# Depthwise stage with partitions ordered (q/k/v, chunk, channel), stores cut to the parts that are read, and constants loaded on GpSimd's queue

## The chip, the cores and the metric

One core of one Trainium2 chip. The metric is the device time of the whole kernel in microseconds, given as the median of several runs. A profiled execution, taken by the hardware profiler, stands beside the runs.

Engines in the text: PE (TensorE), DVE (VectorE), ACT (ScalarE), POOL (GpSimd) and SP (SyncE), which here only issues DMAs. ACT and POOL issue DMAs too.

## The reference

Input x is one image of 48 channels, 256 by 256, in float32. Two layers, each with a residual:

```python
x = x + attention(group_norm(x))
x = x + mix(group_norm(x))

def attention(x):
    qkv = einsum('bchw,oc->bohw', x, w_qkv)        # 48 -> 144 channels
    qkv = depthwise_3x3(qkv, w_dw)
    q, k, v = split(qkv, 3)                        # 48 channels each
    # unfold in 4x4 patches: 64*64 inner patches (and a border of zeros)
    q, k, v = (heads(unfold(t)) for t in (q, k, v))  # 8 heads x 96 x n
    q, k = l2norm(q, over the 96), l2norm(k, over the 96)
    attn = softmax(einsum('bhcn,bhcm->bhnm', q, k) * temperature)
    out = einsum('bhcn,bhnm->bhcm', v, attn)
    return einsum('bchw,oc->bohw', fold(out), w_proj)
```

`mix` multiplies 64 by 64 windows from three sides with three sets of matrices (Ws, Hs, Cs) and adds the three results. A head has 6 channels of q, 6 of k and 6 of v; with the 16 pixels of a patch these are its 96 rows. There are 4096 inner patches, so each head has a 4096 by 4096 attention matrix.

## The kernel before

The kernel runs in stages.

**Head of the kernel.** Constants are loaded (lines 81 to 111): `gm`, `wq`, `wr`, `wp` and `tb` on ACT's queue (14 loads), `dwt`, the depthwise weights, in 21 loads on SP's queue, one for each of 3 parts and 7 chunks. Then x is loaded into SBUF in ten pieces for each half of the image (L424), the upper half on SP and the lower on ACT. DVE takes the statistics of each piece as it arrives (`bn_stats`, L428), then the group norm is folded into `wq` and `wr` and a bias. The pointwise convolution of heads 0 and 1 follows (`pointwise`, L158), and its result is written to a DRAM tensor `t1[0]` (L475). The other six heads' pointwise convolution is done later, in 64 strips of two rows per half (class `Strip`), in the course of head 0's attention; it writes `t1[1]`.

**Depthwise convolution** (class `Depthwise`). For one head h and one step r of ten, 126 partitions hold 7 chunks of the image (index j) times 18 channels of the head: 6 of q, 6 of k, 6 of v. A chunk is 36 image rows; a step takes four of them, with a row above and one below. `load` brings that to the tile `pad`, `first` and `tap` (or `taps_on_tensor`) form the nine taps, `square`, `reduce` and `norm` give the squared norms, summed over the 6 channels of a part by a matmul with the mask `same`; `root` and `scale` divide by them. `nmul` and `nadd` are per-partition constants that give q the temperature and leave v alone. `high` and `low` split the result o in two float32r parts, oh and ol, so that the logits can be computed from three float32r products. `store` writes three tensors to DRAM, `qkv[h][0]` from oh, `qkv[h][1]` from ol and `qkv[h][2]` from o. Each is written with all 126 partitions. Later only q and k are read from the first two (`load_queries`, `load_keys`) and only v from the third (`load_value`). Each partition writes 16 runs of 64 floats.

**Head 0's depthwise stage** (`depthwise_first`) runs alone, before the attention. The pads of steps 0 and 1 are loaded chunk by chunk, alternating between SP and ACT; the other steps with one DMA each on SP. Six of the ten steps have their taps on PE, the other four on DVE. Of their stores oh goes to SP, ol to POOL and o to SP, and for the last two steps oh and ol to SP and o to POOL. The loads of keys and queries for the attention come after these stores, as they read the same DRAM tensor.

**Attention.** A head has 16 groups of two blocks of 128 queries. A block has 48 matmuls for its logits (L344), four exponentials on ACT (L563), and its weighting of the values (`weigh`, L592). The order within a group is written out by hand (`tc.manual_schedule()`). Into it are laid the depthwise steps of the next head, one step in flight in each of the stages `load`/`first`, taps, and `store`; in head 0 also the strips. Pads are loaded on SP, and the three stores are issued on POOL.

**Rest.** After head 7 the projection with the first residual (L739), and then the second layer.

Outside the hand-ordered parts the framework orders each engine's instructions. A DMA has one of eight completion semaphores of the hardware queues (SP and ACT together) or one of eight of POOL's; the next DMA on a semaphore is issued when the one before it has landed.

Of the kernel before, what the change touches and what calls it, by code (L numbers as in the profile page):

```python
# [8 lines left out]
F32 = mybir.dt.float32  # L9
# [11 lines left out]
KS = 4  # L21
KK = KS * KS
NH = 8
HD = C * KK // NH
# [4 lines left out]
CH = 7  # L29
CR = 9  # L30
HC = 3 * C // NH
NP1 = CH * HC
PX = W // KS
H0 = 2
M0 = H0 * HC
# [9 lines left out]
def conv_preact_kernel(  # L45
# [15 lines left out]
    nc = tc.nc  # L61
# [4 lines left out]
    dram = ctx.enter_context(tc.tile_pool(name="dram", bufs=1, space=DRAM))  # L66
# [5 lines left out]
    TR = 2 * CR * KS + (CH - 1) * CR * KS  # L72
    CN = CR * PX
    t1 = [dram.tile([(h1 - h0) * HC, TR, W + 2], F32, name=f"t1_{h0}") for h0, h1 in GROUPS]
    qkv = [dram.tile([3, CH, HC * KK, CN + PX], F32, name=f"qkv{h}") for h in range(NH)]

    os_ = dram.tile([NT // TP, C * KK, TP], F32, name="os_")
    x1s = dram.tile([C, H, W], F32, name="x1s")
# [4 lines left out]
    ones = const.tile([C, 128], F32, name="ones")  # L83
    nc.vector.memset(ones, 1.0)
    gm = const.tile([P2, P2], F32, name="gm")
    nc.scalar.dma_start(out=gm, in_=gmat)

# [3 lines left out]
    wp = const.tile([P2, P2], F32, name="wp")  # L93
    nc.vector.memset(wp, 0.0)
    for s in range(2):
        r = slice(s * C, (s + 1) * C)
        for h in range(NH if s == 0 else H0):
            o = s * M0 + h * HC if h < H0 else (h - H0) * HC
            nc.scalar.dma_start(
                out=(wq[r] if h < H0 else wr[0:C])[:, o : o + HC].rearrange("c (z e) -> c z e", z=3),  # L100
                in_=w_qkvT.rearrange("c (z h e) -> h c z e", z=3, h=NH)[h],
            )
        nc.scalar.dma_start(out=wp[r, r], in_=w_projT)
    dwt = const.tile([NP1, NH, 9], F32, name="dwt")
    dws = w_dw.rearrange("(z h e) i a b -> z e h (i a b)", z=3, h=NH)
    for z in range(3):
        for j in range(CH):
            p = j * HC + z * 6
            nc.sync.dma_start(out=dwt[p : p + 6], in_=dws[z])
    tb = const.tile([1, NH], F32, name="tb")  # L110
    nc.scalar.dma_start(out=tb, in_=temp.rearrange("h a b -> (a b) h"))


    tabs = const.tile([1, 2], F32, name="tabs")
# [55 lines left out]
    class Strip:  # L170
# [5 lines left out]
        def load(self):  # L176
            self.xs = cv.tile([64 + C, 2, W], F32, name="xs", bufs=3)
            for s, rows in enumerate(both_halves(xc, 2 * self.j, 2)):
                nc.sync.dma_start(out=self.xs[s * 64 : s * 64 + C], in_=rows)
# [19 lines left out]
    class Depthwise:  # L199
# [6 lines left out]
        def load(self, engs=None):  # L206
            g = [i for i, (h0, h1) in enumerate(GROUPS) if h0 <= self.h < h1][0]
            c0 = (self.h - GROUPS[g][0]) * HC
            self.pad = self.pool.tile([NP1, KS + 2, W + 2], F32, name="pad", bufs=2 * self.bufs)
            rows = t1[g][c0 : c0 + HC, self.r * KS : self.r * KS + CH * CR * KS, :]  # L210
            rows = rows.rearrange("c (j y) x -> j c y x", j=CH)[:, :, : KS + 2, :]
            if engs:
                for j in range(CH):
                    engs[j % len(engs)].dma_start(out=self.pad[j * HC : (j + 1) * HC], in_=rows[j])
            else:
                nc.sync.dma_start(out=self.pad, in_=rows)

        def first(self):
            self.acc = self.pool.tile([NP1, KS, W], F32, name="acc", bufs=2)
# [79 lines left out]
        def store(self, parts=(0, 1, 2), eng=nc.gpsimd):  # L299
            px = slice(self.r * PX, (self.r + 1) * PX)  # L300
            for i in parts:
                eng.dma_start(  # L302
                    out=qkv[self.h][i].rearrange("j (c k) n -> (j c) k n", k=KK)[:, :, px],
                    in_=self.o if i == 2 else (self.ol if i else self.oh).bitcast(F32),
                )


# [13 lines left out]

    def load_keys(kt, h, m, eng=nc.sync):
        col = m * 512, (m + 1) * 512
        k0, k1 = (qkv[h][i, :, HD : 2 * HD] for i in range(2))
        to = kt.bitcast(F32)
        load(to[0:HD, 0, :], k0, *col, eng)
        load(to[HD:128, 0, :], k1[:, 0:32], *col, eng)
        load(to[0:64, 1, :], k1[:, 32:], *col, eng)
        load(to[64:128, 1, :], k1[:, 32:], *col, eng)

    def load_queries(qt, h, g):
        col = g * 256, (g + 1) * 256
        to = qt.bitcast(F32)
        for i in range(2):
            qi = qkv[h][i, :, 0:HD]
            load(to[0:HD, i, :], qi, *col)
            load(to[HD:128, i, :], qi[:, 0:32], *col)
            load(to[i * 64 : (i + 1) * 64, 2, :], qi[:, 32:], *col)
# [70 lines left out]
    with tc.tile_pool(name="xn", bufs=1) as xnp, tc.tile_pool(name="cst", bufs=1) as cst, tc.tile_pool(  # L409
        name="nps", bufs=2, space=PSUM  # L410
    ) as nps, tc.tile_pool(name="pw", bufs=4, space=PSUM) as pw:
        zr = cst.tile([128, W + 2], F32, name="zr")
        nc.gpsimd.memset(zr, 0.0)
        for (h0, h1), t in zip(GROUPS, t1):
            for y in (0, H + 1):
                nc.gpsimd.dma_start(out=t[:, y, :], in_=zr[: (h1 - h0) * HC])
        xr = xnp.tile([P2, HALF, W], F32, name="xr")
        parts = [16] * 7 + [8, 4, 4]
        st0 = cst.tile([P2, HALF * W // 512, 6], F32, name="st0")
        for i, LR in enumerate(parts):  # L420
            j = sum(parts[:i])
            for s in range(2):
                eng = nc.sync if s == 0 else nc.scalar
                eng.dma_start(  # L424
                    out=xr[s * C : (s + 1) * C, j : j + LR, :], in_=xc[:, s * HALF + j : s * HALF + j + LR, :]
                )
            for i in range(0, LR, 2):
                nc.vector.bn_stats(st0[:, (j + i) // 2, :], xr[:, j + i : j + i + 2, :].rearrange("p a b -> p (a b)"))  # L428
        group_stats(st0, mean0, rstd0, cst, nps)

        nc.vector.tensor_scalar_mul(wq, wq, rstd0)
        nc.vector.tensor_scalar_mul(wr[0:C], wr[0:C], rstd0[0:C])
        nc.gpsimd.dma_start(out=wr[64 : 64 + C], in_=wr[0:C])
        for g, (w, k) in enumerate(((wq, P2), (wr, C))):
            m = w.shape[1]
            pb = nps.tile([128, 1], F32, name="pb0", tag="pstat")
            nc.tensor.matmul(pb[:m], lhsT=w[:k], rhs=mean0[:k], start=True, stop=True)
            nc.vector.tensor_scalar_mul(bias[:m, g : g + 1], pb[:m], -1.0)

        pick = cst.tile([2 * CH, NP1], F32, name="pick")  # L440
        nc.vector.memset(pick, 0.0)
        nc.vector.tensor_copy(
            pick.rearrange("k (j z c) -> k j z c", j=CH, z=3)[:, :, 0:2],
            ident[: 2 * CH, : 2 * CH]
            .rearrange("k (j z u) -> k j z u", j=CH, u=1)
            .to_broadcast([2 * CH, CH, 2, 6]),
        )
        pk = nps.tile([NP1, NP1], F32, name="pk", bufs=1)
        nc.tensor.matmul(pk, lhsT=pick, rhs=pick, start=True, stop=True)
        nc.vector.tensor_copy(same, pk)  # L450
        row = cst.tile([1, NH + 1, NP1], F32, name="row")
        rv = row.rearrange("u i (j z c) -> u i j z c", j=CH, z=3)
        nc.vector.memset(row, 0.0)
        for i in range(NH):
            nc.vector.tensor_copy(
                rv[:, i, :, 0, :], tb[:, i : i + 1].rearrange("u (j c) -> u j c", j=1).to_broadcast([1, CH, 6])
            )
        nc.vector.memset(rv[:, :NH, :, 1, :], 1.0)
        nc.vector.memset(rv[:, NH, :, 2, :], 1.0)
        pr = nps.tile([NP1, NH + 1], F32, name="pr", bufs=1)  # L460
        for i in range(NH + 1):
            nc.tensor.matmul(pr[:, i : i + 1], lhsT=row[:, i, :], rhs=ones[0:1, 0:1], start=True, stop=True)
        nc.vector.tensor_copy(nmul, pr[:, :NH])
        nc.vector.tensor_copy(nadd, pr[:, NH : NH + 1])

        OR = 8
        for y in range(0, HALF, OR):
            ot = xnp.tile([2 * M0, OR, W + 2], F32, name="ot0", bufs=4)
            nc.gpsimd.memset(ot[:, :, 0:1], 0.0)
            nc.gpsimd.memset(ot[:, :, W + 1 : W + 2], 0.0)  # L470
            for i in range(0, OR, 2):
                ps = pw.tile([128, 512], F32, name="pw")
                pointwise(ps, ot[:, i : i + 2, :], xr[:, y + i : y + i + 2, :], on_vector=(i // 2 % 2 == 1))
            for s, rows in enumerate(both_halves(t1[0], y, OR, base=1)):
                nc.sync.dma_start(out=rows, in_=ot[s * M0 : (s + 1) * M0])  # L475
# [11 lines left out]
    with tc.If(nc.values_load(large) > 0):  # L487
# [8 lines left out]
        with tc.tile_pool(name="mk", bufs=NM) as mk, tc.tile_pool(name="mq", bufs=2) as mq, tc.tile_pool(  # L496
            name="mps", bufs=2, space=PSUM
# [23 lines left out]
    with tc.tile_pool(name="ahead", bufs=2) as ah, tc.tile_pool(name="ae", bufs=3) as ae, tc.tile_pool(  # L521
# [15 lines left out]
        def load_value(h, m):  # L537

            vt = ah.tile([HD, 4 * 128], F32, name="vt")
            load(vt, qkv[h][2, :, 2 * HD :], m * 512, (m + 1) * 512)  # L540
            values[h, m] = vt

        def turn(h, m):
# [414 lines left out]
```

## Time and profile before

| | us |
|---|---|
| median of 3 runs | 3771.0 |
| lowest and highest | 3754.03 and 3777.11 |
| the profiled execution's own time | 3774.41 |
| its span, first to last instruction | 3772.6 |
| PE busy | 3521.1 (93%) |
| DVE busy | 2185.9 (58%) |
| ACT busy | 1715.5 (45%) |
| POOL busy | 597.5 (16%) |

A line of the profile's groups or of its timeline names an engine, a line of the kernel and the operation with its output and inputs. Entries with a q after the engine (SPq, ACTq) are DMA issues on that engine's queue. In brackets stands the idle time ahead of an instruction and what ended it. In the table by stage, the last three columns are the granted clock of PE, the mean busy share of the core's 16 DMA engines, and the GB/s that they moved.

### The profile page before, as it was taken

Reading aid. Unit: us, or ns where it says so; the run is one execution under the profiler, and the core shown is the slowest. Engines: PE = TensorE matmul, PEld = TensorE weight load, DVE = VectorE, ACT = ScalarE, POOL = GpSimd, SP = SyncE. Lnnn points to the kernel's source line nnn. Section 1 sums busy time; section 2 is a strip of 40 time slices with the busy share of each in tenths; the row PEclk is TensorE's granted clock in tenths of the full one; section 3 lists DMA queues with packets and bytes.
Section 4 is the critical chain, followed back from the end, with each engine's and each line's share of the span. In section 5 each row is a group of like instructions: output and inputs, shape, how many; then the busy total and the mean of one; then the engine's idle time right before and its main releaser. Section 6 shows DMA issues by size and latency. Waiting matters only on the chain.

```text
span 3772.6 us, 100069 instructions
## 1 busy us (share of the span) xinstructions
PE 3521.1 (93%) x44252; PEld 2916.8 (77%) x44252; DVE 2185.9 (58%) x3514; ACT 1715.5 (45%) x2667; POOL 597.5 (16%) x593
## 2 busy tenths in 40 slices
PE   1877999999999999999999999999999999955998
PEld 0335777788888888888888888888888888812776
DVE  5463675169727962896299439934992222256664
ACT  0224565555545554555455445545554444300222
POOL 0031121012301220122122112211221100010011
PEclk9988999999999999999999999999999999966999
DMA  6575666534433542354245424542543100199784
GB/s 144 170 172 159 178 192 177 166 111 118 114 83 99 126 113 73 104 125 107 84 106 122 101 77 113 119 104 75 125 114 93 46 19 23 31 242 199 128 145 91
DMA packets 307826, 441.64 MB, mean 117 GB/s; under 512 B 98474, under 2 KB 232954, under 8 KB 303160
## 3 DMA queue, kind: packets, MB, share of 16 engines
q1 hardware_dynamic: 253668, 269.65, 27.7%
q0 software_dynamic: 48320, 156.61, 18.5%
q10 hardware_dynamic: 5396, 8.88, 1.1%
q8 instruction: 351, 5.75, 0.7%
q14 instruction: 91, 0.75, 0.1%
HBM read 234.76 MB, written 199.95 MB: 115 GB/s over the span
## 4 chain that ended last, share of the span: by engine, by line
PE 84%; DMA 5%; issue 2%; ACT 0%; SPq 0%; DVE 0%; POOL 0%; ACTq 0%; POOLq 0%
PE big L344 37%; PE big L592 36%; PE pb L856 4%; PE pa L834 2%; PE pc L873 2%; PE big L185 2%; DMA x1s<-pxt 1%; DMA pxt<-in_x_dram 1%; DMA t<-ot 1%; PE pt L609 1%; PE pst L546 1%; PE pn L258 1%; DMA kt<-qkv 0%; DMA os__70<-oo 0%; DMA lxq<-x1s 0%
## 5 line engine op out<-in xcount | busy, mean ns | idle before, releaser
L563 ACT ACTIVATE e<-big,nmx 128x1024 f32<-128x1024 f32 x1024 | 1143.9, 1118 | 833.8 <-PE big L344 622.4
L344 PE MATMUL big<-kt,qt 128*128 128x512 f32 x6144 | 1438.9, 393 | 44.4 <-DMA qt<-qkv 31.6
L592 PEld LDWEIGHTS big<-vn,e 128*64 128x64 f32 x32768 | 1365.8, 137 | 83.4 <-ACT e L563 45.1
L592 PE MATMUL big<-vn,e 128*64 128x96 f32 x32768 | 1423.5, 247 | 5.0 <-ACT ot L188 3.1
L344 PEld LDWEIGHTS big<-kt,qt 128*128 128x128 f32 x6144 | 1145.1, 188 | 307.6 <-issue 46.2
L603 DVE TENSOR_TENSOR oacc<-big,oacc 128x768 f32<-128x768 f32 x480 | 458.1, 954 | 708.5 <-PE big L592 708.5
L239 DVE SCALAR_TENSOR_TENSOR acc<-pad,dwt,acc 126x1024 f32<-126x1024 f32 x592 | 766.2, 1295 | 39.1 <-ACT acc L220 23.5
L297 POOL TENSOR_TENSOR ol<-o,oh 126x1024 fp32r<-126x1024 f32 x78 | 187.1, 2399 | 925.3 <-DVE ss L254 800.9
L576 DVE TENSOR_REDUCE zt<-zs 128x1 f32<-128x4 f32 x256 | 38.9, 152 | 360.4 <-ACT e L563 360.4
L563 ACT ACTIVATION_READ_ACCUMULATOR e<-big,nmx 128x1 f32 x1024 | 196.2, 192 | 0.0
L841 DVE TENSOR_TENSOR lzt<-pa,cbias 128x864 f32<-128x864 f32 (+1 forms) x88 | 137.0, 1628 | 96.9 <-PE pa L834 96.9
L863 ACT COPY lyt<-pb 128x512 f32<-128x512 f32 x144 | 84.5, 586 | 212.9 <-PE pb L856 212.9
L302 POOL DMA_DIRECT2D qkv<-o x72 | 88.6, 1230 | 517.6 <-DVE zu L578 248.9
L613 POOL DMA_DIRECT2D os__70<-oo x128 | 65.2, 515 | 599.6 <-ACT oo L611 598.9
L250 ACT ACTIVATE sq<-acc 126x1024 f32<-126x1024 f32 x74 | 78.2, 1057 | 156.3 <-issue 111.1
L284 DVE TENSOR_TENSOR o<-acc,y 126x1024 f32<-126x1024 f32 x74 | 147.6, 1995 | 0.0
L856 PEld LDWEIGHTS pb<-wsb,lzt 128*64 128x64 f32 x2304 | 125.8, 138 | 27.6 <-issue 19.5
L856 PE MATMUL pb<-wsb,lzt 128*64 128x128 f32 x2304 | 141.7, 279 | 1.3 <-issue 1.3
L188 ACT ACTIVATE ot<-big,bias 108x1024 f32<-108x1024 f32 x64 | 71.1, 1112 | 153.7 <-PE big L185 81.4
L739 PE MATMUL pps<-pot,wp 96*96 96x512 f32 x128 | 78.2, 779 | 58.9 <-DMA pot<-os__70 58.9
L220 ACT ACTIVATE acc<-pad,dwt 126x1024 f32<-126x1024 f32 x74 | 84.1, 1137 | 83.0 <-DMA pad<-t 83.0
L318 POOL DMA_DIRECT2D kt<-qkv x44 | 22.9, 527 | 575.8 <-PE big L344 554.5
(116 smaller groups left out, 1904.5 us busy)
## 6 DMA issues: line engine op xcount, KB each, us to landing
pad<-t SPq DMA_DIRECT2D x78, 761.9 KB
qkv<-ol POOLq DMA_DIRECT2D x78, 504.0 KB, 8.9
qkv<-o POOLq DMA_DIRECT2D x72, 504.0 KB, 6.9
qkv<-oh POOLq DMA_DIRECT2D x70, 504.0 KB, 7.4
t<-ot SPq DMA_DIRECT2D x128, 217.7 KB
qt<-qkv SPq DMA_DIRECT2D x176, 96.0 KB
xs<-in_x_dram SPq DMA_DIRECT2D x128, 96.0 KB
os__70<-oo POOLq DMA_DIRECT2D x128, 96.0 KB, 2.1
```

The costliest lines, as they stand in the source:

```text
L220: nc.scalar.mul(self.acc, self.pad[:, 0:KS, 0:W], dwt[:, self.h, 0:1])
L239: nc.vector.scalar_tensor_tensor(self.acc, self.pad[:, dy : dy + KS, dx : dx + W], dwt[:, self.h, tap : tap + 1], self.acc, ALU.mult, ALU.add,
L284: nc.vector.tensor_tensor(self.o.rearrange("p (a b) x -> p a b x", a=KS), self.acc.rearrange("p a (x b) -> p a b x", b=KS), self.y.rearran ...
L297: eng.tensor_sub(self.ol, self.o, self.oh.bitcast(F32))
L302: eng.dma_start(out=qkv[self.h][i].rearrange("j (c k) n -> (j c) k n", k=KK)[:, :, px], in_=self.o if i == 2 else (self.ol if i else self. ...
L344: nc.tensor.matmul(ps[:, i, :], lhsT=qt[:, r, q0 : q0 + 128], rhs=kts[2 * j + i][:, r // 2, :], start=(r == 0), stop=(r == 2),)
L563: nc.scalar.activation(e[:, j * 1024 : (j + 1) * 1024], ps.rearrange("p a b -> p (a b)"), AF.Exp, bias=nmx[:, b : b + 1], accum_out=zs[:, ...
L592: nc.tensor.matmul(ps[p : p + 64, j // 4, j % 4 * HD : (j % 4 + 1) * HD], lhsT=e[:, mb * 128 + p : mb * 128 + p + 64], rhs=vn, start=(i == 0),
L603: nc.vector.tensor_add(oaccs[h, k], ps[:, :, : 4 * HD], oaccs[h, k])
L841: nc.vector.tensor_tensor(zv[:, :, y0 : y0 + n, :], pa[:, :, : n * T3 * C].rearrange("p s (y k) -> p s y k", y=n), cbias.rearrange("p (u v ...
L856: nc.tensor.matmul(pb[s * WS : (s + 1) * WS, i, :], lhsT=zts[u][:, t * C + c + i, :], rhs=wsb[:, t, :], start=True, stop=True,)
L863: nc.scalar.copy(yt[:, t, :], pb.rearrange("p i x -> p (i x)"))
```

## The change

The partition index changes from (chunk, part, channel) to (part, chunk, channel): q's 42 partitions first, then k's, then v's. So the partitions of q and k are 0 to 83, and those of v 84 to 125. The DRAM tensors get a dimension for the part. `store` writes oh and ol from the first 84 partitions and o from the last 42. `load` of a pad becomes three DMAs, one for each part, or 21 instead of 7 for steps 0 and 1 of head 0. All constants' loads go to POOL's queue.

```diff
+NZ = NP1 // 3
-    qkv = [dram.tile([3, CH, HC * KK, CN + PX], F32, name=f"qkv{h}") for h in range(NH)]
+    qkv = [dram.tile([3, 3, CH, HD, CN + PX], F32, name=f"qkv{h}") for h in range(NH)]
...
-    nc.scalar.dma_start(out=gm, in_=gmat)
+    nc.gpsimd.dma_start(out=gm, in_=gmat)
...
-            nc.scalar.dma_start(
+            nc.gpsimd.dma_start(
                 out=(wq[r] if h < H0 else wr[0:C])[:, o : o + HC].rearrange("c (z e) -> c z e", z=3),
...
-        nc.scalar.dma_start(out=wp[r, r], in_=w_projT)
+        nc.gpsimd.dma_start(out=wp[r, r], in_=w_projT)
...
-            p = j * HC + z * 6
-            nc.sync.dma_start(out=dwt[p : p + 6], in_=dws[z])
+            p = (z * CH + j) * 6
+            nc.gpsimd.dma_start(out=dwt[p : p + 6], in_=dws[z])
...
-    nc.scalar.dma_start(out=tb, in_=temp.rearrange("h a b -> (a b) h"))
+    nc.gpsimd.dma_start(out=tb, in_=temp.rearrange("h a b -> (a b) h"))
...
-            rows = rows.rearrange("c (j y) x -> j c y x", j=CH)[:, :, : KS + 2, :]
-            if engs:
-                for j in range(CH):
-                    engs[j % len(engs)].dma_start(out=self.pad[j * HC : (j + 1) * HC], in_=rows[j])
-            else:
-                nc.sync.dma_start(out=self.pad, in_=rows)
+            rows = rows.rearrange("(z c) (j y) x -> z j c y x", z=3, j=CH)[:, :, :, : KS + 2, :]
+            for z in range(3):
+                if engs:
+                    for j in range(CH):
+                        p = (z * CH + j) * 6
+                        engs[j % len(engs)].dma_start(out=self.pad[p : p + 6], in_=rows[z, j])
+                else:
+                    nc.sync.dma_start(out=self.pad[z * NZ : (z + 1) * NZ], in_=rows[z])
...
             for i in parts:
+                p = slice(2 * NZ, NP1) if i == 2 else slice(0, 2 * NZ)
                 eng.dma_start(
-                    out=qkv[self.h][i].rearrange("j (c k) n -> (j c) k n", k=KK)[:, :, px],
-                    in_=self.o if i == 2 else (self.ol if i else self.oh).bitcast(F32),
+                    out=qkv[self.h][i].rearrange("z j (c k) n -> (z j c) k n", k=KK)[p, :, px],
+                    in_=(self.o if i == 2 else (self.ol if i else self.oh).bitcast(F32))[p],
                 )
...
-        k0, k1 = (qkv[h][i, :, HD : 2 * HD] for i in range(2))
+        k0, k1 = (qkv[h][i, 1] for i in range(2))
...
-            qi = qkv[h][i, :, 0:HD]
+            qi = qkv[h][i, 0]
...
-            load(vt, qkv[h][2, :, 2 * HD :], m * 512, (m + 1) * 512)
+            load(vt, qkv[h][2, 2], m * 512, (m + 1) * 512)
```

The views that fill `pick` (from which `same` is made) and `row` (from which `nmul` and `nadd` are made) are reordered in the same way, with the same instructions.

More of the change, by code (lines that the diff above doesn't have):

```diff
@@ L442, in conv_preact_kernel @@
         nc.vector.tensor_copy(
-            pick.rearrange("k (j z c) -> k j z c", j=CH, z=3)[:, :, 0:2],
+            pick.rearrange("k (z j c) -> k z j c", j=CH, z=3)[:, 0:2],
             ident[: 2 * CH, : 2 * CH]
-            .rearrange("k (j z u) -> k j z u", j=CH, u=1)
-            .to_broadcast([2 * CH, CH, 2, 6]),
+            .rearrange("k (z j u) -> k z j u", j=CH, u=1)
+            .to_broadcast([2 * CH, 2, CH, 6]),
         )
@@ L451, in conv_preact_kernel @@
         row = cst.tile([1, NH + 1, NP1], F32, name="row")
-        rv = row.rearrange("u i (j z c) -> u i j z c", j=CH, z=3)
+        rv = row.rearrange("u i (z j c) -> u i z j c", j=CH, z=3)
         nc.vector.memset(row, 0.0)
@@ L455, in conv_preact_kernel @@
             nc.vector.tensor_copy(
-                rv[:, i, :, 0, :], tb[:, i : i + 1].rearrange("u (j c) -> u j c", j=1).to_broadcast([1, CH, 6])
+                rv[:, i, 0], tb[:, i : i + 1].rearrange("u (j c) -> u j c", j=1).to_broadcast([1, CH, 6])
             )
-        nc.vector.memset(rv[:, :NH, :, 1, :], 1.0)
-        nc.vector.memset(rv[:, NH, :, 2, :], 1.0)
+        nc.vector.memset(rv[:, :NH, 1], 1.0)
+        nc.vector.memset(rv[:, NH, 2], 1.0)
         pr = nps.tile([NP1, NH + 1], F32, name="pr", bufs=1)
```

## The prediction

> **What bounds the kernel now.** I read, in this order, the page's first two parts, PE's waits in the attention, a table by stage over the head of the kernel, and then the timeline there, queue by queue. First the page and PE's waits from 345 to 3310 us:
>
> ```profile
> PE 3521.1 (93%) x44252; PEld 2916.8 (77%) x44252; DVE 2185.9 (58%) x3514; ACT 1715.5 (45%) x2667; POOL 597.5 (16%) x593
> ...
> PE pt L609 <- ACT oo L611: 7.4, 2, 7.1
> PE big L185 <- DMA xs<-in_x_dram: 4.1, 1, 4.1
> PE big L344 <- ACT ot L188: 3.8, 2, 2.1
> ```
>
> From 345 us to the end of the attention PE waits for less than 20 us in total. The change adds or takes no matmul, so nine tenths of the span cannot move. What can move lies before 310 us, and in the few stalls of the first head. The table by stage (columns: stretch, length, busy us and count of PE, PEld, DVE, ACT, POOL, then clock, DMA share, GB/s) and the timeline:
>
> ```profile
> 20.00:40.00 20.00, 0.00 (x0) 0.00 (x0) 10.95 (x19) 0.00 (x0) 0.00 (x0) 1.00 0.99 188
> 40.00:60.00 20.00, 0.00 (x0) 0.00 (x0) 13.26 (x23) 1.28 (x1) 0.00 (x0) 1.00 1.02 215
> ...
> 100.00:120.00 20.00, 20.00 (x48) 6.62 (x47) 8.77 (x12) 7.76 (x12) 0.72 (x10) 1.00 0.58 173
> ...
> 200.00:220.00 20.00, 20.00 (x51) 9.06 (x50) 19.79 (x19) 5.63 (x7) 8.28 (x5) 1.00 0.76 159
> ...
> 260.00:280.00 20.00, 0.08 (x1) 0.00 (x0) 6.05 (x9) 4.04 (x5) 2.44 (x2) 0.51 0.84 178
> ```
>
> ```profile
> 0.73 11.72 SPq L109 DMA_DIRECT2D dwt<-in_w_dw_dram  x21
> 9.82 27.39 ACTq L424 DMA_DIRECT2D xr<-in_x_dram  x7
> 15.65 23.40 SPq L424 DMA_DIRECT2D xr<-in_x_dram  x7
> 68.20 9.59 DVE L428 BATCH_NORM_STATS2 st<-xr 96x6 f32<-96x512 f32 x16 [2.25 <-DMA xr<-in_x_dram]
> ...
> 263.92 2.42 DVE L297 TENSOR_TENSOR ol<-o,oh 126x1024 fp32r<-126x1024 f32 x2
> ...
> 278.39 2.48 SPq L302 DMA_DIRECT2D qkv<-ol  x1
> 286.71 3.03 SPq L318 DMA_DIRECT2D qt<-qkv  x6
> 291.22 0.77 PE L344 MATMUL big<-kt,qt 128*128 128x512 f32 x1 [31.14 <-DMA qt<-qkv]
> ```
>
> To be seen: x is loaded at full DMA share, but its first load is issued only at 9.8 us, behind the constants. From 85 to 143 us PE is the bound (pointwise), from 155 to 257 us PE again (taps of head 0). Then PE stands still for 31 us: DVE writes the last ol at 266.3, but the stores of o, oh and ol are so far behind that the last one is issued at 278.4. The trace's semaphore records have it landing at 284.9, and the first q and k loads go out at 286.2.
>
> [...] The trace agrees: from SP a whole pad load (7 chunks outermost) posts completions from 7 engines, an 18-row pad load from 9, a qkv store (126 partitions) from 14. [...] the small constants' loads took 1.4 to 2.7 us from issue to landing[...]. [...] GpSimd's kt loads took a steady 0.53 us here and its store issues 1.23 us[...].
>
> **The change part by part.** All against the profiled execution, 3774.4 us with a span of 3772.6; it stands 3.4 us over the median of 3771.0, which I lower by the same amount.
>
> *1. Constants on GpSimd.* SP loses 21 dwt loads (0.73 to 12.4 us) and ACT 14 loads (0.73 to 9.8). SP and ACT share eight completion semaphores (every issue on one waits for the landing of the previous), so dwt and x also blocked each other: SP's first x load waited until 15.65. In between only the DMA engines limit: from the first x issue at 9.83 to the last landing at 72.9 is 63.0 us for 12.6 MB. Afterwards x can be issued at 0.75, and shares the engines with the constants, whose whole share in the first 10 us (0.34 and 0.19 of two 5 us slices) is 2.65 us. Last landing 0.75 + 63.0 + 2.65 = 66.4: **6.5 us earlier**. DVE's statistics follow the loads (the last 16, 9.6 us, begin at the arrival of the seventh tile), so they move along. On GpSimd the 35 loads at 0.59 us (its four border stores took 2.35) are 21 us. Queued behind them or between: the memsets of zr and ot (needed at 85) and four border stores (needed at 147), all covered. DVE's temperature chain (tb, 0.3 us plus 4 for the pr matmuls) stands before the statistics: if it stays there, they start near 28 us. They need 64 × 0.605 = 38.7 us and must end at 71.3, so tb may come as late as 28. That cover is thin; bounds of this part: −9 (constants cost nothing) and +9 (eight semaphores each held 9.5 us, as SP's last dwt loads behind x were: 35/8 × 9.5 = 41 us, DVE from 48 to 87).
>
> *2. Pad loads.* The loads of rows 0 and 1 become 42 of 6 partitions instead of 14 of 18. The 18-row ones landed 0.70 us apart with two 6.2 KB rows on each engine. With one row, halving gives 0.35; taking 0.24 per row from the whole loads (4.3 us for 18 rows) leaves 0.22 fixed and gives 0.46. Row 0: 21 × 0.35 to 0.46 = 7.4 to 9.7 instead of 4.9, so PE's first tap at 155.3 comes 2.5 to 4.8 later; I take **+3.5**. If a small load cost a full 0.70, +10. Row 1 and with it rows 2 to 5 come 5 to 9 us later; DVE, which does the odd rows, had 7.3 us of idle between 166 and 246, and PE waited for it at 238 for 2 us, so that stays about level with the 3.5. Later pad loads issue three times on SP (0.73 us before, about 0.45 each) with the same bytes on the same seven engines; ACT's first tap then waits for three landings, with copies and exponentials queued behind it; it idled for a pad only at the start of a head (8 to 9 us), where PE had work all through, but for the first (3.1 us).
>
> *3. Stores.* q and k parts keep 84 partitions, v 42. A row wrote 3 × 126 × 16 = 6048 pieces of 256 B and now writes 3360, 0.556 of it. The 30 stores of head 0 (15.5 MB) ran without a break from 200 to 285; with 8.6 MB they need about 48 us of that rate and keep pace with the rows. What is late next is the computation: ol of row 9 at 266.3 by the old clock. The last two rows' six stores, 1.68 MB at the 174 GB/s of this stage, are 9.7 us from 262.5 on; with completion 274 instead of 284.9: **−11**. Bounds: −16 (the last store lands 3 us after its data; then ACT's table load and e0, done at 273.7, are next) and −6 (the two rows still queue). kt and qt loads to 310 keep their bytes.
>
> *4. First head.* Its PE stalls over 1 us (3.1, 1.7, 4.2, 1.7, 2.1 = 12.7) stand behind t and xs transfers that take 8 to 12 us while the DMA share is 0.64. Stores fall by 0.67 MB per row, out of some 4.7 MB per group; I take a third of the stalls: **−4.5**, bounds 0 and −12.7. In the other heads DMA share is 0.37 and PE is dense: 0. GpSimd's cheaper store issue there saves nothing, its engine is at 16%. The masks (pick, row) and constants only change order: 0.
>
> Sum: −6.5 + 3.5 − 11 − 4.5 = −18.5. 3774.4 − 18.5 = 3755.9; on the median, 3771.0 − 18.5 = 3752.5, given as 3752.
>
> **The rivals.** *A, all covers hold:* constants cost nothing (−9), row 0 +2.5, stores −16, all stalls gone (−12.7): −35, 3736. For it: each stall does end in a DMA. [...] *B, the head gives back:* tb or the small pads stay late (+3 for part 1, +6 for part 2) and only stores and stalls help: +9 − 15.5 = −6.5, 3764. For it: eight semaphores over 35 and 42 loads. *C, slower:* the tripled pad loads take three of SP's eight semaphores instead of one, in the first head where SP issues some 30 transfers per group. SP already waited there 20.1 us in six waits for pad landings before it could issue q loads. If each of the 16 groups then costs a stall like the largest seen, 4.2 us, that is 66 − 12.7 = +53; with −14 for parts 1 to 3, +39, 3810. It decides from 1.7 us of stall per group on (16 × 1.7 = 27 = 12.7 + 14). Against: the three parts land one after the other, so the first semaphore is free sooner than the one of before, and SP's queue has slack (PE's waits above).
>
> **How the numbers follow.** Forecast 0.66, A 0.14, B 0.12, C 0.08. About 1% (37.7 us) is what a measurement of this kernel tells from no change. The range 3728 to 3778 covers the forecast, A and B with the 23 us spread of the runs shown and leaves out C. Faster by over 1% takes A and a favourable spread, 0.11; slower by over 1% is C and what I don't see, 0.09; within 1% 0.80.
>
> **What would show it.** Right: first x issue near 1 us and pointwise matmuls from about 76 instead of 82.4; first tap some 11 us after the last t1 store landed (8 before: 147.4 to 155.3); the last qkv store's issue within 4 us of the last ol, and PE's 31 us gap before the first logits near 20; GpSimd's store issue below 1.23 us; PE dense after 770 as before. Wrong: DVE waiting for tb after 30 us (B), or first-head groups with stalls of 2 us and more at q or xs loads (C).

## The result: 10 us slower, and the profile after

| | before | after |
|---|---|---|
| median of 20 runs each, us | 3771.89 | 3781.74 |
| lowest and highest | 3754.03 and 3788.38 | 3775.39 and 3789.85 |
| the profiled execution's own time | 3774.41 | 3781.40 |
| its span | 3772.6 | 3779.6 |

The ratio after to before is 1.0028, 95% interval 1.0017 to 1.0038. The forecast was 3752, 18.5 us faster, with a range up to 3778. The measured median lies 4 us above the range and on the other side of the kernel before.

First the page's busy times and PE's waits from 345 to 3310 us, as they were read before (engine, tile and line, what it waits for; us in total, times, longest):

```profile
PE 3515.8 (93%) x44252; PEld 2914.0 (77%) x44252; DVE 2187.4 (58%) x3514; ACT 1716.0 (45%) x2667; POOL 547.3 (14%) x628
...
PE pt L613 <- ACT oo L615: 4.5, 1, 4.5
PE big L596 <- DVE vn L586: 1.9, 1, 1.9
PE big L186 <- ACT ot L189: 1.9, 1, 1.9
```

The work of PE, DVE and ACT is the same to 6 us, and the attention's waits for DMAs are gone. So the loss must lie before 310 us again. The table by stage of the kernel after (columns as before) shows where:

```profile
20.00:40.00 20.00, 0.00 (x0) 0.00 (x0) 9.60 (x16) 0.00 (x0) 2.87 (x5) 1.00 1.01 210
40.00:60.00 20.00, 0.00 (x0) 0.00 (x0) 0.00 (x0) 1.28 (x1) 3.94 (x7) 1.00 1.00 217
80.00:100.00 20.00, 0.31 (x2) 0.32 (x2) 19.60 (x31) 0.00 (x0) 0.00 (x0) 1.00 0.00 0
100.00:120.00 20.00, 18.35 (x40) 6.44 (x40) 6.86 (x16) 5.43 (x9) 0.89 (x5) 1.00 0.27 77
200.00:220.00 20.00, 20.00 (x51) 9.08 (x50) 18.45 (x15) 3.12 (x3) 0.00 (x0) 1.00 0.30 114
280.00:300.00 20.00, 8.42 (x23) 3.80 (x21) 8.16 (x11) 3.51 (x5) 6.00 (x6) 0.77 0.63 130
```

From 40 to 60 us DVE does nothing at all, where it had 23 instructions before, although x comes in at the full DMA share. From 80 to 100 it works without a break and the DMA engines stand still: x is there, and the statistics are late. From 200 to 220 the DMAs have fallen from a share of 0.76 to 0.30: the cut stores. The timeline of the kernel after, on the queues of SP and POOL and on DVE and PE, names the wait:

```profile
0.72 49.20 SPq L428 DMA_DIRECT2D xr<-in_x_dram  x10
...
40.10 0.56 POOL L110 DMA_DIRECT2D dwt<-in_w_dw_dram  x1 [3.69 <-DMA wr<-in_w_qkvT_dram]
43.20 0.56 POOL L110 DMA_DIRECT2D dwt<-in_w_dw_dram  x1 [2.54 <-DMA wr<-in_w_qkvT_dram]
...
62.47 5.71 POOL L110 DMA_DIRECT2D dwt<-in_w_dw_dram  x10 [0.52 <-DMA dwt<-in_w_dw_dram]
68.17 0.57 POOL L112 DMA_DIRECT2D tb<-in_temp_dram  x1
69.84 0.15 DVE L116 TENSOR_REDUCE tabs<-tb 1x1 f32<-1x8 f32 x1 [37.26 <-DMA tb<-in_temp_dram]
78.63 19.08 DVE L432 BATCH_NORM_STATS2 st<-xr 96x6 f32<-96x512 f32 x32 [0.26 <-issue]
...
102.56 1.96 PE L159 MATMUL pw<-xr,wq 96*72 96x512 f32 x2
```

x's first load is issued at 0.72, as predicted. But POOL's queue issues one small load per 3 to 4 us, each after a wait for the landing of an earlier one, and `tb` is the last of 35. By the trace's semaphore records the first eight went out by 5.80 us, and the ninth at 12.18, after the first had landed at 11.90. x's loads on SP and ACT waited in the same way: eight were out by 2.14, and the ninth went at 11.24, after the landing of the first at 11.22. DVE waits 37.26 us for `tb`, from 32.6 to 69.84, with 40 of its 64 statistics behind it. The first pointwise matmul comes at 102.56 instead of 82.64.

A second change, one of order, follows in head 0's depthwise stage. The same timeline, ACT and DVE, then SP's last store and the first logits:

```profile
197.63 1.02 ACT L253 ACTIVATE sq<-dps 126x1024 f32<-126x1024 f32 x1 [36.20 <-DMA pad<-t]
198.55 1.14 ACT L223 ACTIVATE acc<-pad,dwt 126x1024 f32<-126x1024 f32 x1
199.88 10.52 DVE L242 SCALAR_TENSOR_TENSOR acc<-pad,dwt,acc 126x1024 f32<-126x1024 f32 x8
...
298.30 2.33 SPq L306 DMA_DIRECT2D qkv<-ol  x1
310.40 0.77 PE L348 MATMUL big<-kt,qt 128*128 128x512 f32 x1 [19.78 <-DMA qt<-qkv]
```

ACT now squares step 0 (`sq<-dps`, which needs PE's taps) before it makes step 1's first tap (`acc`). Step 1's pad had landed at 185.5 by the trace's semaphore records, so `acc` was not held up by data but by the instruction ahead of it. DVE's taps of step 1 start 20.8 us after PE's first tap; before it was 6.1. The store of the last ol follows, and PE's gap before the first logits is 19.78 us instead of 31.14.

The sum over all stages, from the two profiled executions:

| stage | before | after | difference | predicted |
|---|---|---|---|---|
| start to first pointwise matmul | 82.6 | 102.6 | +19.9 | −6.5 |
| to PE's first tap | 72.7 | 76.5 | +3.8 | +3.5 |
| to the end of the last matmul of the norms | 104.7 | 111.6 | +6.8 | 0 |
| to the first logits | 31.1 | 19.8 | −11.4 | −11 |
| to the first weighing | 31.6 | 32.6 | +1.0 | 0 |
| head 0, first weighing to head 1's | 458.2 | 438.4 | −19.8 | −4.5 |
| the rest | 2991.6 | 2998.2 | +6.6 | 0 |

Together +7.0, the difference of the spans. Of the rest, 5.1 us lie in the projection after head 7 (130.6 and 135.7 us). No line of the change touches it, and over the profiles of all kernels here it took 129.9 to 138.1 us, so I put it down to no part.

Head 0's gain is all its stalls. The lengths of its 16 groups, in us from first weighing to first weighing:

```
before 29.6 27.3 27.3 27.3 39.6 27.3 27.3 26.8 26.8 29.2 26.8 31.4 27.4 27.4 27.4 29.3
after  28.5 27.3 27.3 27.3 27.3 27.3 27.3 26.8 26.8 26.8 26.8 27.4 27.4 27.4 27.4 29.3
```

### The profile page after: what moved, and what is told of

It reads as the page before. It is cut to its first block, busy times and chain, and to the rows that moved or that the text cites. A ratio compares the mean times of both kernels' runs of the same rounds, so it can differ in the third digit from the quotient of the medians.

```text
span 3779.6 us, 100418 instructions
## 1 busy us (share of the span) xinstructions
PE 3515.8 (93%) x44252; PEld 2914.0 (77%) x44252; DVE 2187.4 (58%) x3514; ACT 1716.0 (45%) x2667; POOL 547.3 (14%) x628
## 3 DMA queue, kind: packets, MB, share of 16 engines
q1 hardware_dynamic: 234882, 264.80, 26.8%
## 4 chain that ended last, share of the span: by engine, by line
PE 85%; DMA 4%; issue 2%; DVE 0%; ACT 0%; POOL 0%; SPq 0%; POOLq 0%; ACTq 0%
PE big L348 38%; PE big L596 37%; PE pb L860 4%; PE pa L838 2%; PE pc L877 2%; PE big L186 2%; DMA x1s<-pxt 1%; DMA pxt<-in_x_dram 1%; PE pst L550 1%; PE pt L613 1%; PE pn L261 1%; DMA os__70<-oo 0%; DMA lxq<-x1s 0%; DMA kt<-qkv 0%; DVE lzt L845 0%
## 5 line engine op out<-in xcount | busy, mean ns | idle before, releaser
L607 DVE TENSOR_TENSOR oacc<-big,oacc 128x768 f32<-128x768 f32 x480 | 458.2, 955 | 703.0 <-PE big L596 702.8
L306 POOL DMA_DIRECT2D qkv<-o x72 | 56.2, 780 | 525.3 <-DVE zu L582 482.2
L257 DVE TENSOR_REDUCE ss<-sq 126x64 f32<-126x1024 f32 x80 | 97.5, 1219 | 59.2 <-DMA pad<-t 36.4
L231 PE MATMUL dps<-pad,diag 126*126 126x512 f32 x216 | 99.4, 622 | 17.5 <-DMA pad<-t 17.5
```

What stands on the lines that cost most here:

```text
L231: nc.tensor.matmul(ps[:, i, :], lhsT=diag[:, tap, :], rhs=self.pad[:, y : y + 2, dx : dx + W], start=(tap == 0), stop=(tap == 8),)
L257: nc.vector.tensor_reduce(self.ss, self.sq.rearrange("p a (x b) -> p x a b", b=KS), AX.XY, ALU.add)
L607: nc.vector.tensor_add(oaccs[h, k], ps[:, :, : 4 * HD], oaccs[h, k])
```

## The experiments

The runs were taken on three chips, on which the kernel before took 3771.63, 3775.36 and 3771.40 us. Each ratio is to the kernel before on the same chip; a difference of two medians can be off by some 4 us where the chips differ.

### The constants, three ways

The theory (T): the +19.9 is DVE's wait for `tb`, which lands late because it is queued last on POOL, behind 34 loads that the x loads hold up. The rivals: the small loads slow x itself, or POOL's queue as such is slow for `tb`; and for the whole, that the loss comes from the pads.

Constants back on ACT (`wq`, `wr`, `wp` and `tb` as `gm` below) and SP, the rest of the change kept:

```diff
-    nc.gpsimd.dma_start(out=gm, in_=gmat)
+    nc.scalar.dma_start(out=gm, in_=gmat)
-            nc.gpsimd.dma_start(out=dwt[p : p + 6], in_=dws[z])
+            nc.sync.dma_start(out=dwt[p : p + 6], in_=dws[z])
```

> The changed kernel with all constants' loads back on ACT's and SP's queues. Theory T (the change loses its time where DVE waits for tb, queued last on POOL behind 34 loads that the x loads hold up): the first pointwise matmul comes back from 102.3 us to about 82, and the time falls by 20 us and a little, to about 3760, below the kernel before by 12 (stores and first-head stalls keep their gains, pads their loss). Rival P (the small pad loads and the later, three-part ones are what costs): the time stays within 5 us of the changed kernel's 3782.

Measured: 3758.59, ratio to the kernel before 0.9962 (0.9947 to 0.9977), so 23 us less than with the constants on POOL. The first pointwise matmul is at 78.65. ACT's late `acc` stays: DVE's taps start 21.0 us after PE's.

The constants alone on POOL, all 35 of them, in the kernel before:

```diff
-    nc.scalar.dma_start(out=gm, in_=gmat)
+    nc.gpsimd.dma_start(out=gm, in_=gmat)
-            nc.sync.dma_start(out=dwt[p : p + 6], in_=dws[z])
+            nc.gpsimd.dma_start(out=dwt[p : p + 6], in_=dws[z])
```

> The kernel before with nothing changed but the constants' loads, all on POOL's queue. T: first pointwise matmul near 102 us, 20 us later than before, and the time rises by about 20 us to 3792. P: pointwise no later than 82, time 3765 to 3772. If the rest of the change softens the blow (rival: fewer stores give room), the loss here is larger than 20.

Measured: 3796.45, ratio 1.0056 (1.0037 to 1.0076): +25 us by the medians, +21 by the ratio. First pointwise matmul at 104.47, everything after it as before to about 1 us. The wait in its timeline:

```profile
71.82 0.15 DVE L115 TENSOR_REDUCE tabs<-tb 1x1 f32<-1x8 f32 x1 [38.76 <-DMA tb<-in_temp_dram]
```

So this part alone costs more than the whole change, both with the rest and without it. Only `tb` off POOL, first on ACT's queue, in the kernel after:

```diff
+    tb = const.tile([1, NH], F32, name="tb")
+    nc.scalar.dma_start(out=tb, in_=temp.rearrange("h a b -> (a b) h"))
     gm = const.tile([P2, P2], F32, name="gm")
```

> The changed kernel with one load moved: tb is the first load on ACT's queue, the other 34 constants stay on POOL's. T: DVE never waits for tb after 3 us, its statistics follow the x loads, which end near 63, and the first pointwise matmul comes near 70 to 76; the time falls by 26 to 32 us to 3750 to 3756, the lowest so far. Rival Q (35 small loads on POOL beside the x loads slow these themselves, or gm, wq and wr come too late for what needs them at 70 to 80): first pointwise matmul not before 90 and a time of 3770 or more.

Measured: 3755.05, ratio 0.9951 (0.9933 to 0.997), 27 us less than after. One load of 32 bytes moved, and the loss of the other 34 small loads on POOL is gone with it: they are late, but nothing waits. The first matmul, at 79.14, is later than expected; DVE's last statistics, which wait for x and not for `tb`, began at 64.7 in this profile, and x's loading varies, as is taken up below. And `tb` alone on POOL, in the kernel before:

```diff
-    nc.scalar.dma_start(out=tb, in_=temp.rearrange("h a b -> (a b) h"))
+    nc.gpsimd.dma_start(out=tb, in_=temp.rearrange("h a b -> (a b) h"))
```

> The kernel before with tb alone moved to POOL's queue, where nothing is queued ahead of it. If the loss came from tb's place behind 34 loads, and not from POOL's queue as such, tb lands within 4 us, DVE never waits for it, and the time stays at 3771 within 4. If a load on POOL's queue is late by itself beside the x loads, DVE's statistics start after 25 us and the time rises.

Measured: 3776.16, ratio 0.9998 (0.9984 to 1.0012): no loss. From its timeline, `tb`'s use on DVE, then the start of the second pair of pieces of x on DVE:

```profile
3.17 0.15 DVE L115 TENSOR_REDUCE tabs<-tb 1x1 f32<-1x8 f32 x1
...
28.32 4.84 DVE L428 BATCH_NORM_STATS2 st<-xr 96x6 f32<-96x512 f32 x8 [19.20 <-DMA xr<-in_x_dram]
```

On POOL with nothing ahead of it `tb` landed at 3.15 us. What made it late is the queue of 34 loads in front of it, not the queue it is on. In this profile x's loads were late from the start (first pointwise matmul at 90.7), for no reason that the kernel shows.

Nor does DVE's own work explain the late landings: in the kernel after DVE is idle from 32.6 to 69.84 us, and in that time, too, only one small load lands for each piece of x until x ends (the landings are given further below).

### The pads of steps 0 and 1

The theory: 42 small loads instead of 14 made the framework put ACT's square of step 0 ahead of step 1's first tap, and this order is the +6.8. The rival: the small loads' own cost and lateness. In the kernel after with `tb` on ACT, each of the two pads as three loads of 42 partitions:

```diff
-                if engs:
-                    for j in range(CH):
-                        p = (z * CH + j) * 6
-                        engs[j % len(engs)].dma_start(out=self.pad[p : p + 6], in_=rows[z, j])
-                else:
-                    nc.sync.dma_start(out=self.pad[z * NZ : (z + 1) * NZ], in_=rows[z])
+                eng = engs[z % len(engs)] if engs else nc.sync
+                eng.dma_start(out=self.pad[z * NZ : (z + 1) * NZ], in_=rows[z])
```

> The kernel with tb on ACT, and the pads of steps 0 and 1 of head 0 loaded in three DMAs of 42 partitions each, alternating between SP and ACT, instead of 21 of 6. If the 42 small loads cost what the traces suggest, directly (first tap 4 us later than in the kernel before, counted from the first pointwise matmul) and by the order they bring (ACT's square of step 0 ahead of step 1's first tap, so DVE's taps start 20 us after PE's instead of 6), then DVE's taps start within 8 us of PE's, the last norm comes some 8 us earlier and the time falls to 3746 or 3747. Rival: with seven engines for each load the pads come no earlier, and PE's six steps set the end anyway: 3755 as with the small loads.

Measured: 3745.16, ratio 0.9927 (0.9906 to 0.9948). The same kernel with 42 small loads had 0.9951 (0.9933 to 0.997); that is 9 us, but the intervals overlap, and the times alone don't settle it. The stage shows it more clearly: DVE's taps start 4.0 us after PE's first, and the stretch from the first tap to the last norm takes 101.8 us instead of 112.2. To part order from size, step 0 in 21 small loads as in the change, step 1 in three:

```diff
-                if engs:
+                if engs and self.r == 0:
...
                 else:
-                    nc.sync.dma_start(out=self.pad[z * NZ : (z + 1) * NZ], in_=rows[z])
+                    eng = engs[z % len(engs)] if engs else nc.sync
+                    eng.dma_start(out=self.pad[z * NZ : (z + 1) * NZ], in_=rows[z])
```

> The kernel with tb on ACT, step 0's pad in 21 small loads as in the changed kernel, step 1's in three. It parts the small loads' own cost from the order of ACT's instructions that goes with them: here ACT's queue has step 1's first tap ahead of step 0's square again. If the order is what costs (DVE's taps starting 20 us after PE's), DVE starts within 8 us of PE, the last norm comes 102 to 105 us after the first tap instead of 112, and the time is 3746 to 3749, near the three-DMA kernel's 3745. If the small loads themselves cost, through the late first tap, only half of the ten microseconds comes back: 3750 to 3752.

Measured: 3746.04, ratio 0.9942 (0.9921 to 0.9963), which lies between the last two and is told apart from neither. ACT in the timeline of the kernel with 42 small loads (`tb` on ACT), and then in this one:

```profile
173.80 1.02 ACT L253 ACTIVATE sq<-dps 126x1024 f32<-126x1024 f32 x1 [34.83 <-PE dps L231]
174.72 1.14 ACT L223 ACTIVATE acc<-pad,dwt 126x1024 f32<-126x1024 f32 x1
```

```profile
157.83 1.15 ACT L224 ACTIVATE acc<-pad,dwt 126x1024 f32<-126x1024 f32 x1 [22.03 <-DMA pad<-t]
172.37 1.02 ACT L254 ACTIVATE sq<-dps 126x1024 f32<-126x1024 f32 x1 [13.39 <-PE dps L232]
```

The two instructions stand the other way round, and the stretch from the first tap to the last norm is back at 101.9 us, although step 0 is still loaded in 21 pieces. Over all profiles here it took 111.6 to 113.3 us in the four with step 0's square first, and 101.7 to 104.7 in the seven with step 1's tap first.

Two things change together for step 1, though: the order and its loads. In the kernel after, step 1's pad landed 6.4 us after PE's first tap, and `acc` began 13 us later still; here `acc` began 3.4 us after PE's first tap. So up to 3 of the 10 us may come from the earlier data, and a run that changes the order alone is missing. The small loads of step 0 cost something before the first tap: 77.2 us from the first pointwise matmul to it, against 75.5 with three loads. So of the pads' part some 7 to 10 us go with the order and about 2 us with step 0's small loads.

### The stores

All 126 partitions stored again, in the kernel after:

```diff
-                p = slice(2 * NZ, NP1) if i == 2 else slice(0, 2 * NZ)
+                p = slice(0, NP1)
```

> The changed kernel, but all 126 partitions of oh, ol and o are stored again. If the cut stores gave what the two traces suggest (11 us of drain before the first logits, and 19 us over the first head), the time rises by some 30 us to 3812, the gap before the first logits is 31 us again, and the first head has stalls of 2 us and more. If the stores were hidden (the gains come from elsewhere, such as the three-part pad loads), it stays at 3782.

Measured: 3810.55, ratio 1.0095 (1.0073 to 1.0117), 29 us over the kernel after. Its table by stage and its first logits:

```profile
300.00:320.00 20.00, 0.00 (x0) 0.00 (x0) 0.00 (x0) 1.70 (x2) 0.00 (x0) 0.50 0.91 196
```

```profile
327.94 0.77 PE L348 MATMUL big<-kt,qt 128*128 128x512 f32 x1 [34.69 <-DMA kt<-qkv]
```

For 20 us no matmul runs, and the DMAs work at 0.91: the drain is back, 34.7 us against 19.8. Head 0 takes 446.5 us instead of 438.4. So in these two profiles the cut stores are worth 15 us of drain and 8.1 of the 19.8 us gained in head 0; the other 6.7 us between the two spans are spread over the other stages.

### The other part of head 0's gain

The remaining 11.7 us of head 0's gain might come from whole pads that arrive in three parts. In the kernel before, where thirds by part aren't contiguous, the pad was cut by image rows:

```diff
-                nc.sync.dma_start(out=self.pad, in_=rows)
+                for y in range(0, KS + 2, 2):
+                    nc.sync.dma_start(out=self.pad[:, y : y + 2], in_=rows[:, :, y : y + 2])
```

> The kernel before with each whole pad load cut in three DMAs (two image rows of the six each), nothing else. If it is the cut in parts that gave the half of the first head's gain which storing all partitions did not take back (head 0 took 458 us in the kernel before, 446 with all stored, 438 in the changed kernel), head 0 takes 444 to 450 us here and the time is about 3762. If that half came from elsewhere, head 0 stays at 455 to 461 and the time at 3771.

Measured: 3771.19, ratio 0.9992 (0.998 to 1.0003). Head 0 takes 451.4 us, 6.8 less than before, and falls between the two expected ranges. Three profiles of kernels with the old head 0 took 458.2, 457.6 and 455.0 us, so a split like this one is good to about 3 us. Cut loads may have taken some of the stalls away, but the run decides nothing on the 11.7.

### A better version

Three loads per pad as above, `tb` first on ACT, and all other constants on ACT and SP behind the loop that issues x's loads (`wq`, `wr`, `wp` as `gm` below, `dwt` on SP):

```diff
+    tb = const.tile([1, NH], F32, name="tb")
+    nc.scalar.dma_start(out=tb, in_=temp.rearrange("h a b -> (a b) h"))
-    nc.gpsimd.dma_start(out=gm, in_=gmat)
...
+    nc.scalar.dma_start(out=gm, in_=gmat)
```

> The same, with the other constants behind the x loads on ACT's and SP's queues, so that only tb is ahead of x and nothing on POOL's queue runs beside it. If the small loads on a third queue slow x (8.4 us for a pair of pieces with them, 6.9 without), the x loads end near 59 and the first pointwise matmul comes near 72 instead of 79; the time falls by another 6 or 7 us to about 3740. Rival: gm, wq and wr, now issued after 45 us and landing behind x, hold the norm back: first pointwise matmul not before 79, no gain.

Measured: 3739.17, ratio 0.9908 (0.9886 to 0.9929), the fastest of all. It beats the kernel before and the kernel after; against the version with three pad loads and constants on POOL the intervals overlap, and they are not told apart. The expected start of the pointwise matmuls at 72 was missed. DVE's last statistics, in the timeline of this version and then of the one with the constants on POOL:

```profile
61.44 9.58 DVE L412 BATCH_NORM_STATS2 st<-xr 96x6 f32<-96x512 f32 x16 [0.54 <-DMA xr<-in_x_dram]
```

```profile
60.09 9.58 DVE L428 BATCH_NORM_STATS2 st<-xr 96x6 f32<-96x512 f32 x16 [0.44 <-DMA xr<-in_x_dram]
```

Both wait for x, and x is no earlier for having no constants beside it: the first pointwise matmul is at 75.9 and 74.5. A pair of x's large pieces landed every 7.7 us without constants beside it and every 7.5 us with them. What the constants take from x is less than what x's loading varies by from profile to profile.

## Why the prediction was wrong, step by step

**Part 1, constants: the step that failed.** The prediction saw the thin cover ("tb may come as late as 28") and named the mechanism in rival B, but took the cover as holding. The failed step is the pricing of the 35 loads by their issue alone, 0.59 us each and 21 us in all: it lets no load wait for the landing of an earlier one beside x. `tb` was issued at 68.17 us and landed at 69.81. The bound for the case that the cover doesn't hold, 35/8 × 9.5 = 41 us, was too low as well. It took the hold of a semaphore from SP's last dwt loads of the kernel before, which landed 5.8 to 9.7 us after their issue beside the first pieces of x.

In the trace after, the semaphore records show small loads landing at 11.9, 16.6, 20.1, 24.7, 28.0, 32.4, 35.6 and so on up to 57.4, 3.8 us apart on average, while pairs of x pieces landed 7.6 us apart: one small load for each piece of x. At the end of x the pieces are smaller, and the small loads come closer together with them (59.0, 60.5, 61.1, 62.2, 62.8). In all six profiles with the constants on POOL 18 or 19 small loads had landed when the last of x's 20 pieces had. The first 13 took 10.6 to 34.0 us from issue to landing, against 1.4 to 2.7 before. So 13 small loads were through by 57.4 us, five more by the end of x, and the other 17 after it. Why it was one for each piece, the traces don't show.

DVE then did the temperature's chain from 69.84 on and its remaining 40 statistics, and ended them at 97.7, while x was all there by 63.3. The gain expected on x's own side did come: x's last piece landed at 63.3 us, against 72.9 before and 66.4 predicted. In the seven kernels with x at the front it landed at 63.3 to 69.2 us, in the four with x behind constants at 69.4 to 80.9. At the first pointwise matmul, where DVE doesn't wait for `tb`, less of it can be told from the spread: 74.5 to 79.1 us against 78.6 to 90.7.

The prediction's 1.4 to 2.7 us from issue to landing were those of SP's and ACT's loads ahead of x. POOL's last loads here, after x, took 1.6 to 2.0 us.

**Part 2, pads.** The first tap comes +3.8 later, predicted +3.5. The 42 small loads landed 0.38 us apart, inside the 0.35 to 0.46 reckoned. Whole pads, in thirds or not, kept to seven packets at a time: by the trace's packet records just seven were under way in 87% of the time from 160 to 172 us before and in 80% of that from 186 to 200 us after, with three to eight loads outstanding. But with three loads of 42 partitions the tap is still 2 to 3 us later than before (74.7 and 75.5 us after the first pointwise matmul, against 72.7), which the small size of the loads can't explain. So the closeness is in part luck. The step that failed is "stays about level" for DVE's odd rows: +6.8. I reckoned when data arrive and took the order of ACT's instructions as given. The runs showed that the order changed with the number of loads, and that some 7 to 10 us go with it.

**Part 3, stores.** −11.4 measured against −11, and the reason given (the drain) shown by storing all partitions again. (The last two rows' six stores move 1.72 MB, not 1.68, which makes 9.9 us instead of 9.7.) The last store is issued at 298.30. POOL's store issue in the attention takes 780 ns on the page, below the 1.23 us named.

**Part 4, head 0.** The direction was right and the size too small: −19.8 against −4.5, beyond even the bound of −12.7. (A third of 12.7 would be 4.2.) Two terms were mis-sized. Nearly all stalls went and not a third of them; one of 1.9 us is left in the first group. And in one group the stalls cost more than their length. In the kernel before, the fifth group was 12.3 us over its neighbours, though its two waits, 1.69 and 4.15 us, sum to 5.8. The table by stage of the kernel before across it:

```profile
435.00:445.00 10.00, 8.31 (x126) 7.11 (x124) 4.62 (x5) 4.96 (x7) 4.80 (x3) 0.83 0.30 77
445.00:455.00 10.00, 5.85 (x72) 3.60 (x70) 1.83 (x2) 1.11 (x1) 0.00 (x0) 0.82 0.84 216
455.00:465.00 10.00, 10.00 (x81) 7.73 (x81) 5.87 (x17) 2.79 (x3) 0.00 (x0) 0.67 0.68 209
```

The granted clock (third column from the end) falls to 0.83, 0.82 and 0.67, the last in a stretch where PE is busy throughout. The trace's clock records have it at 0.5 from 441.2 to 444.6 us, after a stall of 1.7 us, and from 451.5 to 461.7, after one of 4.2 us began; PE was busy for 12.2 us of that. The group's 329 matmuls kept PE busy for 33.76 us (434.3 to 473.9 us), and the same number in each of the groups beside it for 27.30. These 6.5 us and the 5.8 us of idle time make the 12.3. In the kernel after, the same stretch (425 to 465 us) has no stall, and the clock is 1.00. So in this group the stalls stand once as idle time and again as longer work, with the clock at 0.5 for parts of it. Not every stall was followed by one: after 1.7 us of idle time at 601 the clock records stay at 1.00 until 659.7. What took away the 11.7 us that the stores don't explain is open: the parts of a pad by q, k and v aren't contiguous in the old layout, and the cut by image rows came out between the theories.

**Rivals.** B named both losses, `tb` and the pads, but priced them at +3 and +6; the trace has +19.9 and +10.6 (3.8 + 6.8). C, stalls in each group of head 0, didn't come: groups are at 26.8 to 29.3 throughout.

The prediction also held that only about 1% (37.7 us) can be told from no change. With 20 runs of each kernel the interval was 0.1% to either side, and 10 us were told apart.

## What to carry to other kernels

Before small loads move to another queue beside a bulk transfer, don't price them by their issue alone. In these traces one landed for each piece of the bulk transfer, every 3.8 us, so count them against its pieces. And issue first the load that is needed first: moving one of 32 bytes to the front was worth 27 us here. A change in the number of DMAs can also reorder an engine's compute where the framework sets the order (some 7 to 10 us went with that here), so compare the order of instructions and not only the times at which data land. And when a dense matmul stretch has stalls, their length need not be all that they cost: 5.8 us of them lengthened one group by 12.3 us here.

## What the runs showed of the hardware

- Small loads on POOL's queue beside full-rate loads on SP and ACT landed 3.8 us apart, one for each 768 KB piece of x, and the first 13 of them 10.6 to 34.0 us after issue, against 1.6 to 2.0 us once x had ended.
- 5.8 us of stalls in PE's dense stream lengthened a group by 12.3 us, with a granted clock of 0.5 for 3.4 and for 10.2 us; the same 329 matmuls took 33.8 us of PE's time there and 27.3 in the groups beside it.
- With the same order of loads up to that point the first pointwise matmul came at 74.5, 77.2 and 79.1 us in three profiles, and at 78.6, 78.7 and 82.6 us in three others that load x behind the constants.
